# Two fused transformer layers on one core: inputs of the kept projections asked for one piece ahead, and the first key rotation placed between the two halves of the first norms

## The chip, the cores and the metric

The kernel runs on one core of a Trainium2 chip. The metric is the device time of one execution in microseconds (us), lower being better. The engines are named as in the profile: PE is TensorE (PEld its weight loads), DVE is VectorE, ACT is ScalarE, POOL is GpSimd, SP is the engine that issues most transfers. Each engine works through its own queue in the order of the program.

## The reference

The input has 4 sequences of 1024 tokens with 256 channels. Two layers follow each other; after each half of a layer the result is added to its input and normalised.

```python
x = layernorm(x + attn0(x))     # 16 heads of 16; q and k normalised per head, then rotated
x = layernorm(x + ffn0(x))      # silu(gate) * up, hidden 768, integer weights
x = layernorm(x + attn1(x))     # 8 heads of 32, causal, with a geometric term
x = layernorm(x + moe(x))       # 16 experts (12 with weights), top 2, capacity 512
```

Only the start of the first attention is touched here. There:

```python
qkv = einsum('bsc,oc->bso', x, w_qkv)
q = layer_norm(q, q_gamma, q_beta);  k = layer_norm(k, k_gamma, k_beta)   # over 16 channels
q, k = apply_rope(q, k)
out = softmax(q @ k.T / 4) @ v
```

## The kernel before

Sequences (batches b = 0 to 3) go one after another through four stages; the work is issued in an order written out by hand (`manual_schedule`), so that what stands first in an engine's queue runs first. `tick()` advances a counter, and `later(n, fn)` has `fn` issued n ticks on. `weave(units, n, pieces, ...)` spreads a list of pieces over attention's units of work.

In the first attention the 16 heads form four groups of four. A group needs its queries and keys rotated in token order (`Maxima.rotate`, L396 to L418: six elementwise instructions for each of queries and keys, s = 0 and 1, and each half of the tokens, u = 0 and 1), then transposed (`turn`, L436, giving `qT` and `kT` through an ACT copy at L444), then the maxima of its scores (`head`, L446: matmul L450, reduction L453), and only then the exponentials and the sums over values (`Attend`, L464).

*Start.* `w0` holds the projection weights; columns 0 to 255 serve the heads 0 to 7 (pr = 0), 256 to 511 the heads 8 to 15 (pr = 1), and 512 to 767 the values. `centre(pr)` (L182) takes the mean out of the weights of each head, three DVE instructions, so that the norm needs only a root of the sum of squares. `project_qk(0)` has four pieces of 256 tokens (matmuls L249, squares L257 and copy L258 on ACT, sums L261 on DVE); after every second piece `roots` takes one half of the inverse roots: an addition on DVE (L241), a square root on ACT (L242), a reciprocal on DVE (L243). `straight` issues the pieces in turn. Then group 0 is rotated, with the first keys, (s, u) = (1, 0), on DVE and the other three on POOL:

```python
groups[0] = Maxima(0, 0, {(0, 0): gpsimd, (1, 0): vector, (1, 1): gpsimd, (0, 1): gpsimd})
```

After it come `centre(1)`, the value projection of batch 0 (L282, with ACT copies L289) and the first two transposes.

*Loop of 16 steps.* Each step takes the maxima of one query tile and key half for the four heads of group 0 (`for k, i in enumerate(...)`, L1251), moves group 1's rotation on by four instructions, and takes one piece from `early` or, in steps 8 to 11, from `project_qk(1)`.

*Kept projections.* The projections of batches 1 to 3 are computed ahead and kept in DRAM: `stash_v` (L339) for the values of batches 2 and 3, which make up `early`, and `stash_qk` (L307) for queries and keys. A piece is half of an input of 256 tokens: `load_xin` (L145) asks for the input, 256 KB, on SP's queue at the first half. Its tile has the tag `xin` with two buffers. The matmuls of a piece (L303) go through `bank`, which is the one-buffer pool `ps_m` where `big` is false; ACT copies the result out (L349 or L319), and a store follows on SP (L351; L330 and L331). The value projection of batch 1 isn't kept: it runs at the beginning of batch 1's weave from the same kind of input, in `project_v(1)`.

*Weave and boundary.* `weave(first_units(0), 64, early + stash, ...)` (L1291 on) spreads what is left of the kept projections over batch 0's attention. Then `flush()` issues what is still due, `load_heads(1, 1)` fetches kept queries and keys, eight `load_x` (L525) fetch the rows of batch 1, and batch 1's weave begins with `project_v(1)`.

Of the kernel before, what the change touches and what calls it, by code (L numbers as in the profile page):

```python
# [20 lines left out]
B, S, C = 4, 1024, 256  # L21
# [14 lines left out]
def postln_layers_kernel(ctx: ExitStack, tc: tile.TileContext, a: dict, out: bass.AP):  # L36
# [74 lines left out]
    with ExitStack() as main:  # L111
# [13 lines left out]
        def later(n, fn):  # L125
            due.append((now_at[0] + n, fn))
# [8 lines left out]
        def flush():  # L135
            while due:
                tick()
# [4 lines left out]
                return ps_s.tile([P, 512], F32, tag="s", name=name)  # L142
            return ps_m.tile([P, 512], F32, tag="m", name=name)

        def load_xin(b, j, name):  # L145
            t = fa.tile([P, 2, 256], F32, tag="xin", bufs=2, name=f"xin{name}_{b}_{j}")
            lo = b * S + j * 256
            nc.sync.dma_start(t, a["xT"][:, lo : lo + 256].rearrange("(c p) n -> p c n", p=P))
            return t


# [3 lines left out]
        xin0 = [act.tile([P, 2, 256], F32, tag="pe", bufs=4, name=f"xin0_{j}") for j in range(4)]  # L155
# [26 lines left out]
        def centre(pr):  # L182
            w4 = w0[:, :, pr * 256 : (pr + 1) * 256].rearrange("p c (h d) -> p c h d", h=16)
            nc.vector.tensor_reduce(wsum0, w4, AX.X, ALU.add)
            nc.vector.tensor_scalar_mul(wsum0, wsum0, -1.0 / D0)
            nc.vector.tensor_tensor(w4, w4, wsum0.unsqueeze(3).to_broadcast([P, 2, 16, D0]), ALU.add)

        centre(0)

# [3 lines left out]
        for s in range(2):  # L195
            k = float(D0) ** -0.5 if s == 0 else 1.0
# [33 lines left out]
        def project_qk(pr):  # L230


            b = 0
            xr = fa.tile([P, TB, 2, 8, D0], F32, tag="xr", bufs=1, name=f"xr_{b}_{pr}")
            ss = fa.tile([P, TB, 2, 8], F32, tag="ss", bufs=1, name=f"ss_{b}_{pr}")
            heads[b, pr] = (xr, ss)
            flat = ss.rearrange("p t s h -> p (t s h)")

            def roots(lo, hi):
                r = flat[:, lo:hi]  # L240
                nc.vector.tensor_scalar_add(r, r, D0 * 1e-6)  # L241
                nc.scalar.activation(r, r, AF.Sqrt)  # L242
                nc.vector.reciprocal(r, r)  # L243

            def piece(j, big):
                ps = bank(f"qk0_{b}_{pr}_{j}", big)
                for i in range(2):
                    for c in range(2):
                        nc.tensor.matmul(  # L249
                            ps[:, i * 256 : (i + 1) * 256],  # L250
                            xin0[j][:, c, i * P : (i + 1) * P],
                            w0[:, c, pr * 256 : (pr + 1) * 256],
                            start=c == 0,
                            stop=c == 1,
                        )
                sq = act.tile([P, 512], F32, tag="nmT", bufs=2, name=f"sq0_{b}_{pr}_{j}")
                nc.scalar.activation(sq, ps, AF.Square)  # L257
                nc.scalar.copy(xr[:, 2 * j : 2 * j + 2].rearrange("p t s h d -> p (t s h d)"), ps)  # L258

                def sums():  # L260
                    nc.vector.tensor_reduce(  # L261
                        flat[:, j * 32 : (j + 1) * 32], sq.rearrange("p (h d) -> p h d", d=D0), AX.X, ALU.add
                    )

                if pr:
                    later(1, sums)
                    if j == 3:
                        later(2, lambda: roots(0, 128))
                else:
                    sums()  # L270
                    if j % 2:
                        roots(j // 2 * 64, j // 2 * 64 + 64)

            return [lambda big, j=j: piece(j, big) for j in range(4)]

        def project_v(b):
            def piece(j, big):
                xin = load_xin(b, j, "v") if b else xin0[j]
                ps = bank(f"v0_{b}_{j}", big)
                for i in range(2):  # L280
                    for c in range(2):
                        nc.tensor.matmul(  # L282
                            ps[:, i * 256 : (i + 1) * 256],
                            xin[:, c, i * P : (i + 1) * P],
                            w0[:, c, 512:768],
                            start=c == 0,
                            stop=c == 1,
                        )
                nc.scalar.copy(va0[:, 2 * j : 2 * j + 2, :, 0:D0], ps.rearrange("p (t h d) -> p t h d", t=2, h=H0))  # L289

            return [lambda big, j=j: piece(j, big) for j in range(4)]
# [15 lines left out]
        def stash_qk(b, pr):  # L307
            kept = {}

            def piece(j, i, big):  # L310
                if (j, i) == (0, 0):
                    kept["x"] = act.tile([P, TB * 256], F32, tag="va1", bufs=1, name=f"xs_{b}_{pr}")
                    kept["ss"] = act.tile([P, TB * 16], F32, tag="k1", bufs=G1, name=f"sss_{b}_{pr}")
                if i == 0:
                    kept["in"] = load_xin(b, j, f"k{pr}")
                ps = bank(f"qk0_{b}_{pr}_{j}_{i}", big)
                half(ps, kept["in"], i, slice(pr * 256, (pr + 1) * 256))
                x = kept["x"][:, j * 512 : (j + 1) * 512]
                nc.scalar.copy(x[:, i * 256 : (i + 1) * 256], ps[:, 0:256])  # L319
                if i == 0:  # L320
                    return

                def squares():
                    sq = act.tile([P, 512], F32, tag="q1", bufs=G1, name=f"sqs_{b}_{pr}_{j}")
                    nc.gpsimd.tensor_tensor(sq, x, x, ALU.mult)
                    ss = kept["ss"][:, j * 32 : (j + 1) * 32]
                    later(1, lambda: nc.vector.tensor_reduce(ss, sq.rearrange("p (h d) -> p h d", d=D0), AX.X, ALU.add))

                def store():
                    nc.sync.dma_start(qk_d[b, pr], kept["x"])  # L330
                    nc.sync.dma_start(ss_d[b, pr], kept["ss"])  # L331

                later(1, squares)
                if j == 3:
                    later(3, store)

            return [lambda big, j=j, i=i: piece(j, i, big) for j in range(4) for i in range(2)]

        def stash_v(b):  # L339
            kept = {}  # L340

            def piece(j, i, big):
                if i == 0:
                    kept["in"] = load_xin(b, j, "v")
                    kept["x"] = act.tile([P, 512], F32, tag="nmT", bufs=2, name=f"vs_{b}_{j}")
                ps = bank(f"v0_{b}_{j}_{i}", big)
                half(ps, kept["in"], i, slice(512, 768))
                x = kept["x"]
                nc.scalar.copy(x[:, i * 256 : (i + 1) * 256], ps[:, 0:256])  # L349
                if i == 1:  # L350
                    later(1, lambda: nc.sync.dma_start(v_d[b][:, j * 512 : (j + 1) * 512], x))  # L351

            return [lambda big, j=j, i=i: piece(j, i, big) for j in range(4) for i in range(2)]

        def load_heads(b, pr):

            xr = fa.tile([P, TB, 2, 8, D0], F32, tag="xr", bufs=1, name=f"xr_{b}_{pr}")
            ss = fa.tile([P, TB, 2, 8], F32, tag="ss", bufs=1, name=f"ss_{b}_{pr}")
            heads[b, pr] = (xr, ss)
            flat = ss.rearrange("p t s h -> p (t s h)")  # L360
            nc.sync.dma_start(flat, ss_d[b, pr])
            nc.sync.dma_start(xr.rearrange("p t s h d -> p (t s h d)"), qk_d[b, pr])

            def roots(k):
                if k == 0:
                    nc.gpsimd.tensor_scalar(flat, flat, D0 * 1e-6, None, ALU.add)
                p = flat[:, 16 * k : 16 * k + 16]
                nc.gpsimd.tensor_tensor(p, p, neg_half.to_broadcast([P, 16]), ALU.pow)  # L368

            for k in range(8):  # L370
                later(1 + k, lambda k=k: roots(k))
# [655 lines left out]
        groups = {}  # L1027
# [119 lines left out]
        def straight(pieces):  # L1147
            for k, piece in enumerate(pieces):
                piece(k % 3 != 0)
                tick()  # L1150


        straight(project_qk(0))
        groups[0] = Maxima(
            0, 0, {(0, 0): nc.gpsimd, (1, 0): nc.vector, (1, 1): nc.gpsimd, (0, 1): nc.gpsimd}
        )
        groups[0].rotate()
        centre(1)
        values0 = project_v(0)
        for k in range(3):  # L1160
            values0[k](k != 2)
# [129 lines left out]
            first_units(0), 64, early + stash, False, [lambda big: load_heads(1, 0)], 30, [f for f in prep if f], 0  # L1291
        )
        flush()
        load_heads(1, 1)
        for t in range(TB):
            load_x(1, t)
# [281 lines left out]
```

## Time and profile before

| what | value |
|---|---|
| median of three runs | 2486.8 us (2482.63 to 2492.3) |
| the profiled execution, its own time | 2493.76 us |
| its span | 2492.0 us |
| granted TensorE clock, mean | 0.949 |
| busy: PE, DVE, ACT, POOL | 94%, 56%, 41%, 30% of the span |
| inputs asked for at L148 | 36 of 256 KB; 3.2 and 3.3 us to landing (median, for the kept queries and keys, and for the values) |
| first maxima begin | 24.49 us |
| first scores of the attention proper begin | 88.76 us |
| last kept projection | 382.4 us |

Times of single instructions are counted from the start of the span. A row of the timeline gives the start, the length, the engine, the line, the operation, the output and input tiles, and in brackets how long the engine had been idle before and what ended that. "SPq" is the issue of a transfer by SP's queue, not its landing.

### The profile page before, as it was taken

The page shows a single profiled execution, that of the slowest core. Times are in us where ns is not written, and L with a number is a line of the kernel's source. Part 1 is how long each engine was busy: PE and PEld are TensorE (multiplying, and loading weights), DVE is VectorE, ACT ScalarE, POOL GpSimd, SP SyncE. Part 2 cuts the span into 40 slices and gives each one's busy share as a digit, 9 for nine tenths or more (in the row PEclk, how much of TensorE's full clock was granted, in tenths as well). Part 3 has the DMA queues.
Part 4 walks back from the last instruction along what each step waited for, and adds up shares of the span by engine and source line. Part 5 has one row for each costly group of instructions (what it writes and reads, how often), then busy time and mean ns, then how long its engine had stood idle before and what let it go on. Part 6 is the DMA issues. An engine that isn't in the chain of part 4 may idle for free.

```text
span 2492.0 us, 36155 instructions
## 1 busy us (share of the span) xinstructions
PE 2331.3 (94%) x14004; PEld 1156.8 (46%) x14004; DVE 1384.9 (56%) x3227; ACT 1020.2 (41%) x2037; POOL 743.9 (30%) x1101
## 2 busy tenths in 40 slices
PE   7999998999999999999999999999999974999994
PEld 4433333444444443444444434445556432666662
DVE  6666664766656556686574767806645674111113
ACT  2465554554552445545433464462232231111112
POOL 5234536125204132363051420301112154212223
PEclk9999998999998999999899999998999686999997
DMA  3124212000000000011000000102000012444434
GB/s 96 56 95 143 70 44 70 1 27 1 1 27 1 1 1 1 23 46 33 32 1 1 1 1 1 62 7 99 1 1 1 1 52 69 102 107 114 105 88 146
DMA packets 78124, 107.77 MB, mean 43 GB/s; under 512 B 8832, under 2 KB 67200, under 8 KB 76288
## 3 DMA queue, kind: packets, MB, share of 16 engines
q1 hardware_dynamic: 48592, 73.34, 9.0%
q0 software_dynamic: 9984, 14.82, 3.1%
q10 hardware_dynamic: 19376, 17.30, 2.3%
q8 instruction: 110, 1.80, 0.3%
q14 instruction: 62, 0.51, 0.1%
HBM read 66.54 MB, written 38.90 MB: 42 GB/s over the span
## 4 chain that ended last, share of the span: by engine, by line
PE 86%; DVE 7%; DMA 3%; POOL 2%; issue 1%; ACT 1%; SPq 0%; DVEq 0%; ACTq 0%; POOLq 0%
PE sc L474 19%; PE av L492 10%; PE ph L1439 7%; PE gu L638 7%; PE py L1455 7%; PE sc L964 5%; PE mx L914 4%; PE mx L450 4%; PE p L883 4%; PE dn L654 4%; PE av L1001 3%; PE dn L1001 2%; PE ppa L572 2%; DVE masked L924 2%; PE qk L303 2%; PE pt L441 1%
## 5 line engine op out<-in xcount | busy, mean ns | idle before, releaser
L453 DVE TENSOR_REDUCE part<-mx 128x1 f32<-128x512 f32 x1024 | 655.6, 683 | 338.0 <-PE mx L450 331.7
L483 ACT ACTIVATE pe<-sc 128x512 f32<-128x512 f32 x1024 | 554.2, 596 | 401.5 <-PE mx L450 349.2
L450 PE MATMUL mx<-kT,qT 32*128 32x512 f32 x2048 | 631.4, 646 | 2.1 <-DVE part L453 1.9
L474 PE MATMUL sc<-qT,kT 32*128 32x512 f32 x2048 | 606.4, 639 | 0.0
L474 PEld LDWEIGHTS sc<-qT,kT 32*128 32x128 f32 x2048 | 176.4, 183 | 220.3 <-issue 178.4
L492 PE MATMUL av<-pe,va 128*32 128x512 f32 x2048 | 273.9, 607 | 0.0
L975 ACT ACTIVATE pe<-sc 128x512 f32<-128x512 f32 (+3 forms) x384 | 157.2, 496 | 216.8 <-PE sc L964 216.5
L450 PEld LDWEIGHTS mx<-kT,qT 32*128 32x128 f32 x2048 | 188.2, 185 | 40.0 <-DVE part L453 18.6
L924 DVE CUSTOM_DVE_ANT_0 masked<-mx,mask_w 128x128 bf16<-128x128 f32 (+3 forms) x256 | 125.2, 489 | 122.0 <-PE mx L914 89.8
L1439 PE MATMUL ph<-dmT,f 128*128 128x512 f32 x384 | 170.5, 602 | 4.3 <-DVE dmT L99 3.5
L1447 ACT ACTIVATE hTm<-ph,b 128x512 f32<-128x512 f32 x96 | 60.8, 684 | 261.5 <-PE ph L1439 261.5
L1455 PE MATMUL py<-f,hTm 128*128 128x256 f32 x768 | 167.7, 379 | 0.0
L978 POOL TENSOR_SCALAR_AFFINE_SELECT pe<-pe 128x256 f32<-128x256 f32 x128 | 54.4, 434 | 370.7 <-ACT pe L975 369.2
L1459 POOL DMA_INDIRECT acc_d<-yo,dm x48 | 74.7, 1556 | 285.3 <-DVE yo L1457 233.9
L1455 PEld LDWEIGHTS py<-f,hTm 128*128 128x128 f32 x768 | 145.9, 190 | 25.0 <-issue 5.7
L914 PE MATMUL mx<-kT,qT 32*128 32x512 f32 (+3 forms) x768 | 142.4, 593 | 3.8 <-DVE x L539 3.2
L368 POOL TENSOR_TENSOR ss<-ss,neg_half 128x16 f32<-128x16 f32 x48 | 139.2, 2908 | 0.5
L964 PE MATMUL sc<-qT,kT 32*128 32x512 f32 (+3 forms) x768 | 133.6, 591 | 4.0 <-DVE part L924 2.5
L1456 DVE TENSOR_TENSOR yo<-py,b 128x256 f32<-128x256 f32 x48 | 20.4, 425 | 208.1 <-PE py L1455 208.1
L492 PEld LDWEIGHTS av<-pe,va 128*32 128x32 f32 x2048 | 40.5, 108 | 194.1 <-issue 188.7
L1439 PEld LDWEIGHTS ph<-dmT,f 128*128 128x128 f32 x384 | 72.9, 192 | 95.0 <-issue 86.9
L638 PE MATMUL gu<-xTf,wg 128*128 128x256 f32 x384 | 107.2, 401 | 0.3 <-ACT pe L975 0.3
(346 smaller groups left out, 2976.9 us busy)
## 6 DMA issues: line engine op xcount, KB each, us to landing
f<-in_fc SPq DMA_DIRECT2D x14, 1024.0 KB, 4.9
f<-in_fc ACTq DMA_DIRECT2D x10, 1024.0 KB, 5.9
disp_d<-empty ACTq DMA_DIRECT2D x12, 520.0 KB, 3.4
xink<-in_xT SPq DMA_DIRECT2D x24, 256.0 KB, 3.2
qk_d<-xs SPq DMA_DIRECT2D x6, 1024.0 KB, 3.9
xr<-qk_d SPq DMA_DIRECT2D x6, 1024.0 KB, 6.1
dm<-disp_d SPq DMA_DIRECT2D x11, 520.0 KB, 3.6
x<-in_x SPq DMA_DIRECT2D x32, 128.0 KB, 2.9
```

Source lines behind the costliest of these rows:

```text
L450: nc.tensor.matmul(sc, self.qT[r, t * P : (t + 1) * P], self.kT[r, u * 512 : (u + 1) * 512], start=True, stop=True)
L453: return lambda: nc.vector.tensor_reduce(self.part[:, t, u, h : h + 1], sc, AX.X, ALU.max, negate=True)
L474: nc.tensor.matmul(sc, self.m.kT[r, kt * P : (kt + 1) * P], self.m.qT[r, qb * 512 : (qb + 1) * 512], start=True, stop=True)
L483: nc.scalar.activation(self.pes[i, h // 2][:, h % 2, :], sc, AF.Exp)
L492: nc.tensor.matmul(self.av[32 * h : 32 * h + 32, :], va0[:, kt, 4 * self.g + h, :], self.pes[i, h // 2][:, h % 2, :], start=kt == 0, stop= ...
L638: nc.tensor.matmul(ps[:, i * 256 : (i + 1) * 256], w[:, c, f * P : (f + 1) * P], xT[j][:, c, :], start=c == 0, stop=c == 1,)
L914: nc.tensor.matmul(scs[h][:, :n], qT[r, t * P : (t + 1) * P], kT[r, u * 512 : u * 512 + n], start=True, stop=True,)
L924: nc.vector.tensor_tensor_reduce(masked[:, :n], scs[h][:, :n], mask_w[:, 512 - n :], -1.0, -NEG, ALU.add, ALU.min, part)
L964: nc.tensor.matmul(scs[h][:, off:], ones_h[r, :] if w else kT[r, kt * P : (kt + 1) * P], (self.m.nmT if w else qT)[r, q], start=w == 0, st ...
L975: nc.scalar.activation(pe[:, j, off:], scs[2 * hp + j][:, off:], AF.Exp)
L1439: nc.tensor.matmul(ph[:, i * CAP : (i + 1) * CAP], f1[:, c, (f + i) * P : (f + i + 1) * P], dmT[:, c, :], start=c == 0, stop=c == 1,)
L1455: nc.tensor.matmul(py[:, :C], hT[:, f, c * P : (c + 1) * P], f2[:, f, :], start=f == 0, stop=f == FF1 // P - 1)
```

## The change

`load_xin` is replaced by two functions and a list that names all 36 inputs in the order of their use. `load_ahead` asks for the next input on the list; `take_xin` hands over the oldest that has been asked for and, where none is left waiting, asks for the next. The first `load_ahead` stands before `project_qk(0)`, and one more stands after `flush()`; `project_v(1)` asks for another after the matmuls of each piece. `centre(1)` moves up to directly behind `centre(0)`. The four pieces of `project_qk(0)` are issued two by two, and twelve steps of group 0's rotation (the first queries on POOL, the first keys on DVE) are issued between them. As `straight` chooses the bank by a piece's place in its list, pieces 2 and 3 take the banks `ps_m` and `ps_s` instead of `ps_s` and `ps_m`.

```diff
-        def load_xin(b, j, name):
+        xin_next = [(b, j, "v") for b in (2, 3) for j in range(4)]
+        xin_next += [(b, j, f"k{pr}") for b in range(1, B) for pr in range(2) for j in range(4)]
+        xin_next += [(1, j, "v") for j in range(4)]
+        xin_here = []
+
+        def load_ahead():
+            b, j, name = xin_next.pop(0)
             t = fa.tile([P, 2, 256], F32, tag="xin", bufs=2, name=f"xin{name}_{b}_{j}")
             lo = b * S + j * 256
             nc.sync.dma_start(t, a["xT"][:, lo : lo + 256].rearrange("(c p) n -> p c n", p=P))
+            xin_here.append(((b, j, name), t))
+
+        def take_xin(b, j, name):
+            key, t = xin_here.pop(0)
+            assert key == (b, j, name)
+            if xin_next and not xin_here:
+                load_ahead()
             return t
...
         centre(0)
+        centre(1)
...
         # project_v
-                xin = load_xin(b, j, "v") if b else xin0[j]
+                xin = take_xin(b, j, "v") if b else xin0[j]
...
+                if b and xin_next:
+                    load_ahead()
                 nc.scalar.copy(va0[:, 2 * j : 2 * j + 2, :, 0:D0], ps.rearrange("p (t h d) -> p t h d", t=2, h=H0))
...
         # stash_qk
-                    kept["in"] = load_xin(b, j, f"k{pr}")
+                    kept["in"] = take_xin(b, j, f"k{pr}")
...
         # stash_v
-                    kept["in"] = load_xin(b, j, "v")
+                    kept["in"] = take_xin(b, j, "v")
...
-        straight(project_qk(0))
+        load_ahead()
+        first = project_qk(0)
+        straight(first[:2])
         groups[0] = Maxima(
             0, 0, {(0, 0): nc.gpsimd, (1, 0): nc.vector, (1, 1): nc.gpsimd, (0, 1): nc.gpsimd}
         )
+        groups[0].rotate(12)
+        straight(first[2:])
         groups[0].rotate()
-        centre(1)
         values0 = project_v(0)
...
         flush()
+        load_ahead()
         load_heads(1, 1)
```

## The prediction

> **What bounds the kernel now.** I read the shares of busy time first: TensorE (PE) is busy 94% of the 2492.0 us, and 86% of the chain that ended last runs over it. So a change pays where TensorE stands still. The view of what TensorE waited for (total, times, longest) names the transfers this change touches:
>
> ```profile
> PE v L303 <- DMA xinv<-in_xT: 13.2, 4, 4.4
> PE v L282 <- DMA xinv<-in_xT: 8.8, 1, 8.8
> PE qk L303 <- DMA xink<-in_xT: 5.5, 4, 1.9
> ```
>
> Together 27.5 us in nine waits, all for the 256 KB inputs that `load_xin` (L148) asks for. Next the stages (columns: stretch and length, busy us of PE, PEld, DVE, ACT, POOL, granted TensorE clock, DMA share, GB/s): start, loop of 16 maxima steps, weave of batch 0's attention, boundary to batch 1, what follows.
>
> ```profile
> 0.00:24.50 24.50, 16.78 (x74) 14.11 (x74) 16.91 (x46) 8.81 (x17) 18.11 (x39) 1.00 0.62 159
> 24.50:88.80 64.30, 50.38 (x241) 26.41 (x240) 42.65 (x71) 13.10 (x28) 15.70 (x27) 0.87 0.14 42
> 88.80:383.40 294.60, 287.86 (x1861) 105.86 (x1860) 191.47 (x325) 174.98 (x340) 117.56 (x155) 0.99 0.25 85
> 383.40:403.30 19.90, 11.12 (x49) 4.59 (x48) 5.30 (x10) 4.86 (x10) 15.64 (x10) 0.66 0.61 204
> 403.30:480.00 76.70, 76.70 (x499) 33.07 (x496) 51.98 (x103) 42.78 (x80) 32.60 (x42) 1.00 0.02 4
> ```
>
> Loop and boundary are the two stretches with idle TensorE and a clock below 0.9. After 403.3 TensorE is full at clock 1.00, so what is saved earlier moves everything later forward. The timeline shows why a load is late (start, length, engine, line; in brackets the idle time before it):
>
> ```profile
> 38.13 0.37 ACT L349 COPY vs<-v 128x256 f32<-128x256 f32 x1 [2.90 <-PE v L303]
> 38.53 0.33 SPq L351 DMA_DIRECT2D v_d<-vs  x1
> 38.96 0.38 SPq L148 DMA_DIRECT2D xinv<-in_xT  x1
> ...
> 42.45 1.10 PE L303 MATMUL v<-w,xinv 128*128 128x256 f32 x4 [3.18 <-DMA xinv<-in_xT]
> ...
> 51.59 2.05 PE L303 MATMUL v<-w,xinv 128*128 128x256 f32 x4 [3.51 <-DMA xinv<-in_xT]
> ```
>
> The load stands in SP's queue behind a store that waits for ScalarE's copy of the piece before; it goes out 0.4 us after that copy, and the next piece stands 3.2 us. The second buffer is free all along. After the 51.59 wait the same four matmuls take 2.05 instead of 1.10 us.
>
> [...] the load above, itself free to go, leaves only after the store ahead of it. [...] here waits of 2.2, 3.5, 4.4 and 8.8 us were followed by doubled matmul times and one of 3.2 us was not.
>
> **Part 1, loads one piece ahead.** No DMA, byte or matmul is added; 36 issues (24 xink, 12 xinv, about 0.4 us of SP each) move forward. `take_xin` emits the next load when a piece begins, two loop steps (over 4 us) before it is needed; landing takes 3.2 us (median). Its buffer's last reader is the piece before, already done, and the store now ahead of it on SP is one piece older, so it waits for nothing current. SP is idle between these issues. The very first load passes the 14 loads of L1168 to L1224 (14.90 to about 6.5 us) and delays each by 0.4 us; the earliest use of those is in the weave, so nothing.
>
> *Loop, steps 2 to 8* start at 29.10 and 57.59: 28.5 us. Without waits: a plain step is bound by DVE's four reductions, 2.48 us, and was 2.48 where no load was late (26.62 to 29.10). Two of the six steps have a transpose as well, whose copy shares the one bank of `ps_m`; one without a wait took 3.46 (43.48 to 46.94). 4 x 2.5 + 2 x 3.46 = 16.9. **Saved 11.6.**
>
> *Loop, steps 14 and 15*, 75.70 to 88.76 = 13.1 us, with a 4.4 us wait and about 2.9 us of half-clock matmuls behind it (2.05, 2.09, 1.11, 1.67 for 1.10, 1.14, 0.66, 1.10). Without: step 14 is held by DVE (0.21 + 0.95 + 2.41 with a root on ACT between, 4.3), step 15 by PE (1.1 + 0.65 + 1.1 = 2.9). 7.2. **Saved 5.9.**
>
> *Weave*: 5.5 us of xink waits and 1.17 us ahead of 105.53, where the load landed that moment. All have two units (9 us) of cover afterwards. **Saved 6.7.**
>
> *Boundary.* The first v input of batch 1 is emitted behind two head loads and eight x loads:
>
> ```profile
> 387.35 5.77 SPq L525 DMA_DIRECT2D x<-in_x  x8
> ...
> 393.25 13.53 SPq L148 DMA_DIRECT2D xinv<-in_xT  x4
> ...
> 396.50 3.78 PE L282 MATMUL v<-w,xinv 128*128 128x256 f32 x8 [8.78 <-DMA xinv<-in_xT]
> ...
> 404.39 1.99 PE L282 MATMUL v<-w,xinv 128*128 128x256 f32 x8
> ```
>
> Afterwards input 0 is asked for at the last kept piece (some 373 us here) and input 1 after the flush, ahead of the heads; these lose 0.4 us. Input 2 queues behind the x loads (393.5, landing about 397) for a piece at about 398: just covered. Saved: 8.8 of wait, 1.8 of cold v matmuls (3.78 for 1.99), 1.0 of the next half-clock unit (402.23 - 400.21 for 1.04). What is late next is POOL: its roots and additions (L368, L527) run to 406.2 whatever TensorE does, then 28 us of rotation; that now ends near 435, for transposes near 444. **Saved 11.6.**
>
> **Part 2, the start.** `centre(1)` (three DVE instructions, 0.67 + 0.41 + 0.69) moves from 22.05, where DVE idled anyway, to behind `centre(0)`, where DVE idles 1.26 us (6.5 to 7.75) waiting for gamma. Its weights should land near 6.5 (issued 2.30, median landing 4.2): end about 8.4, ropes 0.7 us later (0.5 if the weights are early, 1.5 if late). The key rotation (six DVE instructions, 18.42 to 22.12 = 3.7 us) now comes ahead of the sums of pieces 2 and 3:
>
> ```profile
> 17.66 0.26 ACT L242 ACTIVATE ss<-ss 128x64 f32<-128x64 f32 x1 [0.72 <-DVE ss L241]
> 17.82 0.57 ACT L289 COPY va<-v 128x512 f32<-128x512 f32 x1
> ...
> 22.18 0.65 PE L441 MATMUL pt<-ident,tokk 128*128 128x128 f32 x4 [1.19 <-DVE tokk L417]
> 22.67 1.89 PE L282 MATMUL v<-w,xin 128*128 128x256 f32 x8
> ```
>
> DVE: the first roots end at 15.6 + 0.7 = 16.3, rotation 16.3 to 20.0, sums (2 x 0.67), L241 0.41: 21.7; before, tokk stood at 22.1. So the transpose can go 2 us earlier. But the second root (L242) now reaches ACT at 21.7 instead of 17.66, and behind it in ACT's order stand three value copies and the copies of qT and kT (five of 0.5 to 0.6): qT and kT end at about 24.7, not 23.46. The fourth value projection waits for the bank freed by the third copy (23.6), takes 1.9, and the first maxima start at about 25.6 instead of 24.49. **Lost 1.1.** POOL's second halves get their roots at 22.6, not 18.5: about 3 us late, group 1's rotation ends near 44 instead of 41.3, for a buffer wanted at about 50. The order of `ps_m` and `ps_s` banks for pieces 2 and 3 changes; both are long free. Bounds of the whole part: a gain of 1 (copies tighter than written) to a loss of 4 (TensorE idles 2 us from 21.6 and goes cold: 1.9 more for the projection, 1 for the first maxima).
>
> **Sum.** -11.6 - 5.9 - 6.7 - 11.6 + 1.1 = -34.7. The profiled execution took 2493.8 (span 2492.0 and 1.8 around it), 7.0 above the median of the three runs. 2493.8 - 34.7 = 2459.1 against it; against 2486.8, **2452**.
>
> **Rivals.**
> 1. *Waits turn into others* (0.22). The kept pieces share one `ps_m` bank with the transposes, and ACT empties it; a new wait of 0.5 us per step over 16 steps costs 8, a cold start 3 more: gain 24, or 2463. For it: bank waits of 0.7 to 1.2 us on ACT are in the trace. Against: steps without a late load took 2.1 to 2.5 us.
> 2. *The loads don't get ahead* (0.04): SP's order or the two buffers hold each issue where it was. Only the start's +1.1 is left: 2488. Against: between 15.3 and 29.6 SP issues nothing, and the buffers alternate.
> 3. *Slower: the clock* (0.04). From 403 on TensorE has about 1965 us of work. If fewer pauses bring the granted clock down, each percent costs 20 us; from 1.8% on the gain is gone, 3% give 2486.8 - 34.7 + 59 = 2511. Against: from 403.3 to 480 TensorE is 100% busy at 1.00.
>
> **Numbers.** The forecast has 0.70, its own spread 2444 to 2459: terms unknown by a few us, run to run 5. Rival 1 takes the range to 2467. A measurement can tell 0.5% (12 us) from no change: faster 0.92 (forecast and rival 1), same 0.04 (rival 2), slower 0.04 (rival 3).
>
> **What would show it.** No wait of TensorE for xink or xinv above 1 us; loop from first maxima to the first score about 47 us, not 64; its clock near 1; each load in the loop leaving SP two steps before its matmuls; boundary v matmuls at about 1.9 us without a gap. The start is right if L242's second root sits near 21.7 with five ACT copies behind it. Wrong: waits of like size on ACT's copies or DVE's reductions in the loop, or first maxima after 29.

## The result, and the profile after

The changed kernel took 2455.1 us (median of four executions, 2445.8 to 2456.6); the kernel before took 2489.2 beside it. The ratio is 0.9856, with a 95% interval of 0.9832 to 0.9881: 1.4% faster. The profiled execution spans 2454.4 us against 2492.0. In the code after the change, `load_ahead` issues at L155, the matmuls of the kept pieces stand at L320, their ACT copy at L366, the store at L368, the first maxima at L467 and the value projection at L297.

The view of what TensorE waited for (total, times, longest) no longer has any of the three rows of before. Of these two rows the first is new, and the second is what is left of the waits for inputs:

```profile
PE v L297 <- ACT va L306: 2.3, 1, 2.3
PE v L297 <- DMA xinv<-in_xT: 1.7, 1, 1.7
```

No wait for xink is left, and of 22.0 us for xinv only 1.7. The 8.8 us of before and this 1.7 stand at the same place, the boundary between batches 0 and 1, but not at the same input. The stages of the changed kernel (start, loop, weave, boundary, what follows; the columns are those of before):

```profile
0.00:25.40 25.40, 16.59 (x76) 14.00 (x76) 15.26 (x46) 8.50 (x17) 16.66 (x38) 1.00 0.60 163
25.40:71.80 46.40, 44.88 (x237) 24.66 (x236) 41.81 (x71) 13.09 (x28) 16.61 (x29) 1.00 0.19 58
71.80:359.40 287.60, 286.79 (x1861) 105.50 (x1860) 191.98 (x325) 174.13 (x340) 117.17 (x155) 1.00 0.26 87
359.40:367.60 8.20, 8.20 (x49) 3.27 (x48) 5.19 (x10) 4.74 (x10) 2.94 (x3) 1.00 0.80 264
367.60:446.00 78.40, 76.67 (x499) 33.03 (x496) 52.70 (x103) 42.77 (x80) 45.23 (x49) 1.00 0.08 25
```

Read the second row: the loop takes 46.4 us instead of 64.3, its DVE work is the same (41.8 busy, 42.7 before), and it now fills 90% of the loop. TensorE's busy time fell too, from 50.4 to 44.9 us for the same work, because the granted clock (the share of full speed at which TensorE was let run) rose from 0.87 to 1.00. The fourth row is the boundary: 8.2 us with the same 49 matmul records that took 19.9.

In the timeline of the loop, the order on SP looks as before, store first and load after it, and the first store still leaves only when ACT's copy has ended (30.45):

```profile
30.08 0.37 ACT L366 COPY vs<-v 128x256 f32<-128x256 f32 x1 [2.05 <-PE v L320]
30.48 0.33 SPq L368 DMA_DIRECT2D v_d<-vs  x1
30.91 0.38 SPq L155 DMA_DIRECT2D xinv<-in_xT  x1
...
36.33 0.33 SPq L368 DMA_DIRECT2D v_d<-vs  x1
36.76 0.38 SPq L155 DMA_DIRECT2D xinv<-in_xT  x1
```

and TensorE's own timeline shows that the load is that of a later input:

```profile
37.25 1.13 PE L320 MATMUL v<-w,xinv 128*128 128x256 f32 x4
...
45.59 1.13 PE L320 MATMUL v<-w,xinv 128*128 128x256 f32 x4
```

The matmuls at 37.25 start 0.5 us after a load was issued, too soon to be fed by it, since an input took at least 2.9 us to land in the loop: they use the one issued at 30.91, and the load of 36.76 is that of the pieces from 43.10 on. Both loads leave 6.3 us before their matmuls begin, and none of these waits for an input.

Landmarks, from which the rest is worked out:

| landmark, us | before | after |
|---|---|---|
| first maxima | 24.49 | 25.36 |
| loop step 2 | 29.10 | 29.97 |
| loop step 8 | 57.59 | 46.65 |
| loop step 14 | 75.70 | 64.97 |
| first scores | 88.76 | 71.81 |
| last kept projection | 382.39 | 358.37 |
| fourth value matmul of batch 1 | 415.10 | 381.17 |
| end of the span | 2492.0 | 2454.4 |

At 381.17 the changed kernel is 33.9 us ahead. The last 3.7 of the 37.6 us come later, in stages that the change doesn't touch.

### The profile page after: what moved, and what is told of

It is laid out like the page before. It is cut to its first block, busy times and chain, and to the rows that moved or that the text cites. A ratio compares the mean times of both kernels' runs of the same rounds, so it can differ in the third digit from the quotient of the medians.

```text
span 2454.4 us, 36158 instructions
## 1 busy us (share of the span) xinstructions
PE 2317.0 (94%) x14004; PEld 1150.6 (47%) x14004; DVE 1385.0 (56%) x3227; ACT 1018.4 (41%) x2037; POOL 741.7 (30%) x1101
## 4 chain that ended last, share of the span: by engine, by line
PE 87%; DVE 8%; DMA 1%; POOL 1%; issue 1%; ACT 1%; SPq 0%; DVEq 0%; POOLq 0%; ACTq 0%
PE sc L491 20%; PE av L509 10%; PE ph L1460 7%; PE gu L655 7%; PE py L1476 7%; PE sc L981 5%; PE mx L931 4%; PE mx L467 4%; PE p L900 4%; PE dn L671 4%; PE av L1018 3%; PE dn L1018 2%; DVE masked L941 2%; PE ppa L589 2%; PE qk L320 2%; PE pt L458 1%
## 5 line engine op out<-in xcount | busy, mean ns | idle before, releaser
L467 PE MATMUL mx<-kT,qT 32*128 32x512 f32 x2048 | 630.5, 638 | 2.1 <-DVE part L470 1.9
L467 PEld LDWEIGHTS mx<-kT,qT 32*128 32x128 f32 x2048 | 189.2, 183 | 40.2 <-DVE part L470 21.2
```

Of the source, the lines that this page charges most:

```text
L467: nc.tensor.matmul(sc, self.qT[r, t * P : (t + 1) * P], self.kT[r, u * 512 : (u + 1) * 512], start=True, stop=True)
```

## The experiments

**The loads alone**: the changed kernel with the old start.

```diff
         centre(0)
-        centre(1)
...
-        first = project_qk(0)
-        straight(first[:2])
+        straight(project_qk(0))
         groups[0] = Maxima(...)
-        groups[0].rotate(12)
-        straight(first[2:])
         groups[0].rotate()
+        centre(1)
```

> The changed loads alone, with the start as before (centre(1) behind the rotation, all four pieces of the norms in one go). Theory (the gain comes from the loads, the new start costs about 1 us): first maxima at 24.5 us as before, first scores at about 70.9 (the changed kernel: 71.8), boundary as in the changed kernel, 35 us less than before, about 2454. Rival (the earlier rotation is what keeps the loop fed): the loop stays longer than in the changed kernel by several us, first scores after 75, gain under 30.

Measured: first maxima at 24.44, first scores at 70.88, fourth value matmul of batch 1 at 379.39, which is 35.7 less than before. The time was 2445.8 us, ratio 0.9836 (0.981 to 0.9863). The loop is as long as in the changed kernel (46.4 us), so the earlier rotation does nothing for it. The rival falls. That the total is 9 us below the changed kernel was not expected; it is taken up below.

**The start alone**: the kernel before with the new start.

> The changed start alone, with each input asked for at its use as before. Theory (queues of DVE and ACT): first maxima at 25.4 us against 24.49, first scores at about 89.7 against 88.76, all later waits as before, time within 2 us of before, a loss of about 1. Rival (the earlier keys help the loop): first scores before 87, a gain of 2 us or more.

Measured: first maxima at 25.00, first scores at 89.00, ratio 0.9995 (0.9981 to 1.0008). The new start costs 0.5 us at the first maxima and 0.2 at the first scores in this profile, too little for the time to show. The rival, a gain, falls.

**The store one tick later**, in the kernel before:

```diff
-                    later(1, lambda: nc.sync.dma_start(v_d[b][:, j * 512 : (j + 1) * 512], x))
+                    later(2, lambda: nc.sync.dma_start(v_d[b][:, j * 512 : (j + 1) * 512], x))
```

> The kernel before, with one change: the store of kept values is issued two ticks after its copy instead of one, so that in SP's queue the next load stands ahead of it. No load is asked for earlier in the program. Theory (head of the queue: the load was late only because a store that waits for ScalarE stood before it): the 13.2 us of TensorE's waits for xinv in the loop go to under 1, first scores at about 71, and the waits of the weave (5.5) and the boundary (8.8) stay; about 17 us less than before, 2472. Rival (what counts is asking a piece ahead in the program): over half of the 13.2 us stays and the time falls by 8 us at most.

Measured: first scores at 70.77, 18.0 us earlier than before, and 2466.8 us, ratio 0.9917 (0.9892 to 0.9942). The 21.6 us in all are 4.6 more than said; at the last kept projection it is 21.0 ahead (361.34). Its waits of TensorE, in the first 420 us:

```profile
PE v L282 <- DMA xinv<-in_xT: 8.7, 1, 8.7
...
PE qk L303 <- DMA xink<-in_xT: 5.4, 4, 1.9
```

The row of 13.2 us for the loop is gone, though every load is still written where it is used; the other two rows stand as they were. SP's queue shows how:

```profile
14.89 1.05 SPq L148 DMA_DIRECT2D xinv<-in_xT  x2
29.45 0.34 SPq L351 DMA_DIRECT2D v_d<-vs  x1
29.90 0.37 SPq L148 DMA_DIRECT2D xinv<-in_xT  x1
```

The second input now leaves right behind the first, ahead of the first store; before, it left at 29.98, behind that store. From there on each load stands behind the store of an input one earlier than before, which is the order on SP that the changed kernel has too. One digit in the store's delay brings the whole of the loop's 18 us, and the loop is as long as in the changed kernel (46.4 us). This settles the cause in the loop: not the place in the program at which the input is asked for, but which store stands ahead of its load in SP's queue. For the waits of the weave and of batch 1's first input no run moves the queue's order alone; these went when the loads were moved.

**The centring back** behind the rotation, in the changed kernel.

> The changed kernel with centre(1) back behind group 0's rotation; loads and split norms as changed. Theory (the early centring delays the whole DVE chain, since its weights land at 7.9 us and gamma at 7.75): DVE's second root addition 1.6 us earlier than the 21.43 of the changed kernel, about 19.8, and first maxima at about 23.8 against 25.36. Rival (ACT and TensorE set the start, the centring fills an idle slot): first maxima at 25.2 or later.

Measured: the second root's addition at 20.53, first maxima at 24.87. Both came earlier, by 0.9 and 0.5 us, but not by the 1.6 of the theory. The one execution took 2455.7 us. In this run the second piece of the norms also reached ACT later than in the changed kernel (13.16 against 11.69), which took half of DVE's lead away. The changed kernel itself had its first maxima at 25.36, 25.10 and 25.00 in three profiles, so 0.5 us is no more than such a difference. The price of the early centring stays open; between 0 and 1 us is an estimate from these differences.

**Copies ahead of the second root**, in the changed kernel: the roots of pieces 2 and 3 are issued behind the first three value projections.

```diff
+        second_half = []
...
-                    if j % 2:
-                        roots(j // 2 * 64, j // 2 * 64 + 64)
+                    if j == 1:
+                        roots(0, 64)
+                    elif j == 3:
+                        second_half.append(lambda: roots(64, 128))
...
         straight(first[2:])
-        groups[0].rotate()
         values0 = project_v(0)
         for k in range(3):
             values0[k](k != 2)
+        second_half.pop()()
+        groups[0].rotate()
```

> The changed kernel, with the second half's roots issued behind the first three value projections, so that ACT's three value copies stand ahead of the second square root. Theory (the new start lost its lead because the second root, late on DVE, heads ACT's queue): no wait of TensorE for a value copy before the fourth value projection (2.3 us in the changed kernel), kT copied at about 23.2 and first maxima at about 23.3 against 25.36; first scores about 70. Rival (DVE's chain or TensorE's own order holds the start): first maxima after 24.5.

Measured: no wait for a value copy, kT copied at 23.19, first maxima at 24.05, first scores at 70.5. The wait is gone, as the theory has it; of the 2 us it gave 1.3 against the changed kernel's first profile, and 1.0 against its latest one. In this run TensorE's first transpose came at 21.28, 1.2 us later than in that first profile; in the run with both orders (below) it came at 20.65, and the same start had its first maxima at 23.42. The one execution took 2444.1 us. How the root holds the start is plain in the changed kernel's timeline, DVE, ACT and TensorE together:

```profile
21.43 0.22 DVE L256 TENSOR_SCALAR ss<-ss 128x64 f32<-128x64 f32 x1
21.68 0.26 ACT L257 ACTIVATE ss<-ss 128x64 f32<-128x64 f32 x1 [3.29 <-DVE ss L256]
21.84 1.54 ACT L306 COPY va<-v 128x512 f32<-128x512 f32 x3
...
23.26 0.61 ACT L461 COPY qT<-pt 128x512 f32<-128x512 f32 x1
...
23.44 2.00 PE L297 MATMUL v<-w,xin 128*128 128x256 f32 x8 [2.28 <-ACT va L306]
...
25.36 1.14 PE L467 MATMUL mx<-kT,qT 32*128 32x512 f32 x8
```

ACT stands idle for 3.3 us while three projections that it has to copy are finished (the third by 20.28), since the root ahead of them waits for DVE; TensorE stands 2.3 us for the bank that the third copy frees. With both orders changed, the same stretch reads:

```profile
20.85 0.59 ACT L310 COPY va<-v 128x512 f32<-128x512 f32 x1 [1.14 <-PE v L301]
...
21.48 0.26 ACT L259 ACTIVATE ss<-ss 128x64 f32<-128x64 f32 x1
21.52 1.96 PE L301 MATMUL v<-w,xin 128*128 128x256 f32 x8
...
23.42 1.14 PE L471 MATMUL mx<-kT,qT 32*128 32x512 f32 x8
```

The third copy ends before the root begins, and TensorE goes on without a wait.

**Row loads behind input 2**, in the changed kernel:

```diff
         load_heads(1, 1)
-        for t in range(TB):
-            load_x(1, t)
-        weave(first_units(1), 64, ..., [lambda big: load_heads(2, 0)], 30)
+        weave(first_units(1), 64, ..., [lambda big: load_heads(2, 0)], 30,
+              [lambda t=t: load_x(1, t) for t in range(TB)], 1, 2)
```

> The changed kernel, with batch 1's eight row loads (load_x) issued two per unit from the weave's second unit on, behind input 2 of the values instead of ahead of it. Theory (the 1.7 us wait left at the boundary is the eight row loads standing ahead in SP's queue): that wait goes to 0, the value matmuls of pieces 2 and 3 each follow the one before by 5.1 to 5.7 us. Rival (the load waits for its buffer or for the DMA's own time): a wait over 1 us stays. Either way under 2 us of the total, and POOL's rotation still ends ahead of its transposes.

The wait that this goes for is, in the changed kernel, on SP and on TensorE:

```profile
363.86 7.15 SPq L542 DMA_DIRECT2D x<-in_x  x8
371.11 2.03 SPq L155 DMA_DIRECT2D xinv<-in_xT  x2
```

```profile
368.69 2.00 PE L297 MATMUL v<-w,xinv 128*128 128x256 f32 x8
...
375.55 1.97 PE L297 MATMUL v<-w,xinv 128*128 128x256 f32 x8 [1.73 <-DMA xinv<-in_xT]
```

Measured, the value matmuls of batch 1 with the rows behind:

```profile
361.60 1.99 PE L297 MATMUL v<-w,xinv 128*128 128x256 f32 x8
366.66 1.99 PE L297 MATMUL v<-w,xinv 128*128 128x256 f32 x8
371.72 1.99 PE L297 MATMUL v<-w,xinv 128*128 128x256 f32 x8
377.37 1.99 PE L297 MATMUL v<-w,xinv 128*128 128x256 f32 x8
```

No wait is left; the steps are 5.1, 5.1 and 5.7 us. Input 2 goes out 2.0 us behind the first matmul's start (363.62) and not 7.5. The theory holds, though the wait that was there to win varies: in two later profiles of the changed kernel it was 0.7 and 1.1 us. The time, one execution, was 2451.5 us.

**Both orders together**, and **the changed kernel again** beside it, five rounds each.

> The changed kernel with the two orders above, value copies ahead of the second root and row loads behind input 2. Theory: the two add, about 4 us less than the changed kernel up to the fourth value matmul of batch 1 (381.2 there, about 377 here) and 2451 in all; the rest differs with the granted clock only. Rival: one of the two waits turns up elsewhere before that point, and less than 2 us are left.

> The changed kernel again, on the same chip as the variants. Expected near 2455, with the fourth value matmul of batch 1 at 381 us as before. If the later part (beyond 420 us) differs from the first profile by several us at the same order of instructions, the granted clock moves it and not the change.

Measured: the fourth value matmul of batch 1 at 377.20 with both and at 379.69 in the changed kernel's new profile (381.17 in its first). Against the first profile that is the 4 us of the theory; against the one beside it, it is 2.5: 1.7 at the first maxima (23.42 and 25.10) and 0.8 at the boundary, where the wait in that profile was only 0.7. So more than the rival's 2 us is left, but the forecast of 4 holds against one profile only. The times can't confirm it: 2447.4 us, ratio 0.9855 (0.9833 to 0.9878), against 2455.8, ratio 0.9873 (0.9849 to 0.9897). Each of the two kernels spreads over 14 to 19 us, and its single times follow the mean granted clock: the changed kernel took 2440.1 and 2440.8 at 0.965, and 2455.1 to 2459.2 at 0.955 to 0.957.

**The old start again, with and without the rows behind, and the changed kernel a third time**, five rounds each.

> The changed loads with the old start, again. In its first four executions it took 2440 to 2449 us at a mean granted clock of 0.962 to 0.966; the changed kernel took 2440 to 2459 at 0.955 to 0.965 in ten. Theory (each execution falls at random into a higher or a lower granted clock in the waits after 420 us): now some executions near 2455 at 0.957 as well. Rival (the old start leads to the higher clock each time): all near 2444 at 0.963 or more.

> The changed loads with the old start and the eight row loads behind input 2. Up to the fourth value matmul of batch 1, 1.9 us less than with the changed loads alone (379.4 there), about 377.5, with no wait for an input. In all 1 to 2 us less where the granted clock is the same, and not to be told apart by time.

> The changed kernel once more on the same chip as the two. Theory (random): a mix of about 2440 and about 2456, as in the ten executions before. Rival (the new start leads to the lower clock): most near 2456 while the kernels with the old start stay near 2444.

Measured: the loads alone 2445.7 us, ratio 0.9827 (0.9815 to 0.984), all between 2442.9 and 2447.7. The loads alone with the rows behind 2442.7, ratio 0.9815 (0.9802 to 0.9827), all between 2441.3 and 2444.4, no wait for an input left, the fourth value matmul at 379.50 and not 377.5: the boundary is 2.0 us shorter than in the first profile of the loads alone, as forecast, but the first maxima came 0.5 later (24.97) and the weave took 1.6 more. The changed kernel 2451.8, ratio 0.9858 (0.9833 to 0.9882), between 2443.1 and 2462.4. The rival is right as far as the old start goes: 14 executions with the changed loads and the old start lie within 2440 and 2449, while 16 of the changed kernel spread over 2440 to 2462, five of them below 2449. Between these last two profiles, 2442.7 and 2451.7 us long, the difference lies in one stretch of the last weave. Here are 40 us of it at the same distance from the last gate projection, first in the changed kernel (its first profile; the third has the same clock there), then in the loads with the rows behind:

```profile
1897.00:1937.00 40.00, 39.41 (x220) 18.88 (x216) 24.37 (x68) 8.17 (x21) 5.42 (x14) 0.63 0.00 1
```

```profile
1896.00:1936.00 40.00, 38.34 (x285) 18.66 (x285) 30.29 (x89) 13.13 (x31) 5.86 (x15) 0.96 0.01 1
```

TensorE is busy throughout in both, but at a granted clock of 0.63 it gets through 220 matmul records and at 0.96 through 285. From the last gate projection to the last output projection the loads alone took 197.9 us in both profiles, and so did the loads with the rows behind; the changed kernel took 208.0, 203.2 and 207.9. The kernel before, with the old start too, took 209.7. So the old start doesn't by itself keep the clock up. Nor does the new start fix one length: in all thirteen profiles the stretch has one of three lengths, 197.9 (the three just named), 203.2 and 203.3 (the changed kernel's second and the copies ahead of the second root) and 207.7 to 209.9 (the other eight). This stretch is not the whole of the scatter either: from the fourth value matmul to the last gate projection the six profiles of the changed kernel and of the changed loads with the old start took 1433.1 to 1444.8, and the shortest span of all (2438.3) is the changed kernel's second. What ties the clock in this stretch to the order of the first 25 us was not found; the length of the stretch goes with the granted clock (0.63 and 0.96 above, and 0.76 at the same place in the profile with 203.2), and that is shown; why the clock differs is open.

The version to keep is the changed loads with the old start, whose single times lie between 2440 and 2449 in both of its runs. With the rows behind input 2 its interval lies below that of the changed kernel in the same run, but it overlaps that of the loads alone (0.9802 to 0.9827 against 0.9815 to 0.984), so that the rows' own gain is seen at the boundary and not in the time.

## Why the prediction was right, step by step

It gave 2452 us, with a spread of its own from 2444 to 2459 and up to 2467 with the first rival, and 2455.1 came. Its steps against the landmarks:

| step | forecast, us | measured, us |
|---|---|---|
| start | +1.1 | +0.9 |
| loop, steps 2 to 8 | -11.6 | -11.8 |
| loop, steps 8 to 14 | 0 | +0.2 |
| loop, steps 14 and 15 | -5.9 | -6.2 |
| weave | -6.7 | -7.1 |
| boundary | -11.6 | -9.9 |
| sum to the fourth value matmul | -34.7 | -33.9 |
| after that | 0 | -3.7 in this profile |

- *Loop.* Without late loads a plain step took 2.13 to 2.49 us and one with a transpose 3.73 and 3.72 (29.97 to 33.70, 38.31 to 42.03); taken were 2.5 and 3.46. The two misses cancel by luck: steps 2 to 8 took 16.7 for 16.9. That DVE bound it, by its reductions for the most part, shows in the loop's row, 41.8 busy of 46.4. Steps 14 and 15 took 3.4 each, where 4.3 and 2.9 were said; here too only the sum was met. The doubled matmul times behind the waits were rightly counted as part of the stall: in the kernel before, the four matmuls of a piece took 2.05 us behind the waits of 3.51 and 4.38 us; in the changed kernel each such piece of the loop took 1.03 to 1.13 us, and the loop's clock went from 0.87 to 1.00 as the waits went.
- *Queue order.* The store one tick later shows by itself that a store which waited for ScalarE's copy held back a later load of the same queue: the second input left at 29.98 behind the first store (29.61), and by 15.94 with that store behind it. One reason in the prediction was wrong: the store now ahead of a load "waits for nothing current". It still waits for the copy that has just ended (30.45, store 30.48, load 30.91). The load is in time because it belongs to an input that is needed 6.3 us later, and landing took 2.9 to 3.3 us in the loop.
- *Boundary.* The step that failed is "input 2 queues behind the x loads (393.5, landing about 397) for a piece at about 398: just covered". The eight row loads took 7.15 us to issue instead of 5.77, input 2 left at 371.11, it landed 4.3 us later, where 3.5 was reckoned, and its piece stood 1.7 us. So one of the prediction's own signs, no wait above 1 us, didn't come. Everything up to there is -11.7, as forecast. POOL's rotation ended at 411.0, ahead of the first of its transposes at 422.7.
- *Start.* The chain was the forecast one: roots on ACT at 21.68 (21.7 said), five copies behind, fourth projection at 23.44 (23.6), first maxima at 25.36 (25.6). The centred weights landed at 7.9, not at 6.5, so the ropes began 1.7 us later and not 0.7; DVE's rotation was shorter than before (16.96 to 20.21, 3.3 for 3.7), and so the sum held, again with misses that cancel. In the two later profiles the first maxima came at 25.10 and 25.00, so that the loss was 0.5 to 0.9 us. Behind its wait of 2.28 us TensorE took 2.00 us for the fourth projection and 1.14 for the first maxima, at a granted clock of 1.00 (23.44 to 26.50), so the doubled times in the prediction's bound of a loss of 4 us did not come. In the kernel before, a wait of 2.18 us was followed by first 1.50 us for four matmuls and then 2.09 for eight that took 1.14 elsewhere; what decides between the two was not shown.
- *The clock.* The loss that rival 3 feared didn't come: the mean granted clock was 0.958 in the profiled execution, against 0.949 before. That fewer pauses bring the clock down was an assumption of the prediction. But the scatter was put too low, at 5 us from run to run: with one and the same order of instructions, single executions of the changed kernel took 2440.1 to 2462.4 us, a difference larger than any term of the sum. The landmarks up to the fourth value matmul confirm the sum; that the median of four came within 3 us of 2452 is in part luck.

## What to carry to other kernels

Look at what stands ahead of a late load in its queue before moving the load: here a store that waited for ScalarE's copy held back a load that was free to go (in the kernel before it left at 38.96, the copy having ended at 38.50, and TensorE stood 3.18 us for it), and delaying the store by one step brought the loop's 18.0 us. Ask, for a step that is moved on one engine, what it will hold up in the queues of the others: here a square root that waited for DVE kept ScalarE idle for 3.3 us ahead of three copies, and TensorE stood 2.3 us for the last of them. Where single executions differ by more than the change is worth, compare landmarks of the profile ahead of the place where they part.

## What the runs showed of the hardware that was not expected

A stretch in which TensorE had hardly any idle time ran at well below full clock: 39.4 us busy in 40 at a granted clock of 0.63, with no wait above 0.4 us, in the kernel before and in the changed one. The profile models the ends of matmuls, so this says that TensorE was hardly ever left without an instruction, not how full it was. The same 40 us of the kernel before:

```profile
1932.00:1972.00 40.00, 39.41 (x224) 18.93 (x224) 24.66 (x69) 8.60 (x22) 5.04 (x13) 0.63 0.00 1
```

Of its 224 matmul records 200 belong to the second attention; the mean length of one is 0.3 to 1.1 us, by shape. The same stretch ran at 0.96 in three profiles with the old start and the changed loads, where TensorE was busy 38.3 us of 40: so its busy share hardly tells the two apart, and the granted clock does. What brings the clock down there was not found.
